# Transfers through DRAM in one piece, transposes that write with a stride, and a planner that counts transfers

## Chip, cores and metric

The kernel runs on one core of one Trainium2 chip. The metric is the device time in microseconds; "before" is the median of three runs. One more execution was taken with the hardware profiler, and all durations below come from it. TensorE (PE in the profile) multiplies; VectorE (DVE), ScalarE (ACT) and GpSimd (POOL) do elementwise work; SyncE (SP) issues nearly all DMAs.

## The reference

There are 128 graphs of 128 nodes with 512 features (`x`) and a weighted adjacency matrix each (`adj`, 128 x 128), all fp32. Four residual layers follow one another, each with a layer norm:

```
x = layernorm(x + L0(x, adj))   # T = row-normalised adj * exp(leaky_relu(s_j + s_i)); relu(x W0 + T x W1 + T T x W2 + b)
x = layernorm(x + L1(x, adj))   # hypergraph conv 512 -> 1024, relu, layer norm, hypergraph conv 1024 -> 512, plus x
x = layernorm(x + L2(x, adj))   # F = row-normalised exp(act(8 tanh(s_i + s_j))) * adj, times row sums of adj; F x W
x = layernorm(x + L3(x, adj))   # attention with 8 heads, scores times (adj + adj), output projection
```

Layer 0 needs T transposed, layer 1 needs adj and its hidden activations `h` transposed, layer 2 needs F transposed, layer 3 needs its input `x3` and the attention weights `S` transposed[...].

## The kernel before

The graphs are taken in 64 pairs (`U = 2`); a job of `layer0`, `layer1` or `layer23` works on two pairs. Weight products are done by a seven-product scheme (`strassen`, nested in `twice`); each product accumulates in a PSUM bank (`bank`, or `t0`, `t1`), which VectorE or ScalarE then adds or copies into SBUF before the bank is written again.

Nothing is issued in the order of the program text. Every call (`pe.matmul`, `ve.transpose`, `sp.dma_start` and so on) is recorded by `Plan.add` with a price in ns from `estimate`, a key (the layer's stage times `WHEN0`, `WHENT`, `WHENH` and the like) and its dependencies. `Plan.order` then plays the five engines forward in a list schedule: it gives tiles their buffers, lets an operation begin when its inputs and a buffer are there, counts `ISSUE` = 450 ns of SyncE for a DMA, and makes transfers follow one another through one pipe. `Plan.deadlines` works due times back from TensorE's starts, and `emit` plays the schedule up to two times more with these as ranks of all engines but TensorE, keeps the shortest, and emits every engine's instructions in that order. Each engine then runs its list in order. `plan.together(share)` makes one operation of several calls, at `share` of the summed price. As `emit` makes all calls at one line, the profile has almost everything under L375; operations are told apart by tile and shape.

A 128 x 128 transpose that isn't done on TensorE takes two steps. `through_dram` stores the source into a DRAM scratch tile, cut into four column blocks of 32 (index `k`), and its `load()` reads it back so that partition `32 k + r` holds column block `k` of some rows; `from_dram` does such a read directly from an input. Then `turned` transposes 32 x 32 blocks on VectorE. Rows come in the order `(m r)`: row 32 m + r, with four groups `m`.

- With `in_order=True` (`e` in layer 0, `h` in layer 1, `x3` in layer 3, whose scratch tiles the profile calls `e`, `h` and `x`) the store is issued in four DMAs of 32 partitions each per block `j`, so that DRAM holds rows as `k r m j w` and the loaded row is 32 m + r.
- With `False` (`F` in layer 2, `S` in attention) it is one DMA of 128 partitions per `j`; the load takes `(r m)`, row 4 r + m, and the rows are put in order later, when ScalarE copies the product out of PSUM (`rows_in_order`). The last attention job, whose `S` does not go through DRAM, is brought into that order by ScalarE copies that write with `"p (i m r) -> p i r m"`.
- `from_dram` (`x` in layer 0, `adj` in layer 1) issues four DMAs of 32 partitions for each of the two graphs of a pair, into `p m j w`.

Every transpose writes 32 neighbouring elements in a run. The functions that the change touches follow, with the line numbers of the profile.

Of the kernel before, what the change touches and what calls it, by code (L numbers as in the profile page):

```python
# [17 lines left out]
P = 128  # L18
D = 512
C = D // P  # L20
Q = 32
# [5 lines left out]
U = 2  # L27
# [33 lines left out]

LATENCY = ((0, 205, 215, 255, 300), (225, 120, 110, 200, 200), (160, 145, 140, 200, 200), (110, 140, 100, 105, 200),
           (2300, 2300, 2300, 2300, 2300))
ISSUE, BEGIN = 450, 1000
EARLY = -0.5
QW = 3 * P + 2
SLACK = 60
SPARE, AHEAD = 4, 6
YIELD = 20
SIZE = {"four": U * D, "sq": U * (P + 2), "bank": D, "col": 12, "row": D, "w28": 7168, "q7": 7 * 2 * P,  # L70
        "w7": 7 * QW, "out": U * 4 * QW, "t0": D, "t1": D, "row1": 4 * D, "k": U * (P + 2),
        "prep": U * D}
# [51 lines left out]
def estimate(engine, name, out, args, kw):  # L124

    n = out.idx.size if isinstance(out, View) else 0
    views = [a for a in args if isinstance(a, View)]
    psum = any(a.tile.kind in PSUM for a in views)
    scalars = sum(isinstance(a, View) and a.idx.size == 1 for k, a in [*enumerate(args), *kw.items()] if k != "accum_out")
    if engine == PE:  # L130
        return 107 if name == "transpose" else (1.74 if n <= P else 1.68) * n
    if name == "dma_start":
        return ISSUE
    if engine == DVE:
        if name == "bn_aggr":
            return 95
        if name == "reciprocal":
            return 67 + 6.5 * n
        if name in ("tensor_reduce", "bn_stats"):
            n = views[0].idx.size  # L140
        fast = name in ("tensor_scalar", "tensor_copy") and not psum and "accum_out" not in kw
        return 67 + n / (1.92 if fast else .96) + (61 * scalars if n > 8 else 0)
    if engine == ACT:
        return 50 + n / 1.2 + (0 if psum else 43) + 92 * scalars + 94 * ("accum_out" in kw)
    if name == "tensor_tensor":
        return 500 + 35 * n if OP.pow in args else 150 + 2.1 * n if n < 800 else 1.82 * n
    return 60 if name == "memset" else 180 + 3.2 * n if n > 8 else 215


def shares_port(engine, name, args, kw):  # L150
# [22 lines left out]
class Plan:  # L173
# [64 lines left out]
    def order(self, urgent=None):  # L238


        ops = self.ops
# [30 lines left out]
        come, free, start = [0.0] * n, [0.0] * 5, [0.0] * n  # L272
        port = [0.0] * 5
        pipe, reached = 0.0, EARLY
        for k in range(n):
            if not left[k]:
                ready[ops[k][0]][k] = 0.0

        def look(e):

            can = []
            soonest = math.inf
            for k, t in ready[e].items():
                if e == SP and ops[k][8] > reached and not ops[k][4]:
                    continue
                t = max(t, free[e], port[e] if ops[k][6] else 0)
                new = {}
                for tile in ops[k][5]:
                    if tile not in place:
                        new.setdefault(tile.kind, []).append(tile)  # L290
                for kind, tiles in new.items():
                    s, m = slots[kind], len(tiles)
                    spare = 0
                    if not all(tile in line[kind][-m:] for tile in tiles):
                        spare = SPARE if all(tile in line[kind][-m - AHEAD:] for tile in tiles) else math.inf
                    if len(s) < m + (min(spare, 4) if kind == "bank" else spare):
                        break
                    t = max(t, sorted(s)[m - 1][0])
                else:
                    can.append((rank[k], t, k))  # L300
                    if t < soonest:
                        soonest = t
            if not can:
                return None
            r, t, k = min(c for c in can if c[1] <= soonest + SLACK)
            return t, k
# [3 lines left out]
        while count < n:  # L310
# [15 lines left out]
            free[e] = end = t + o[2]  # L326
            if o[7]:
                end = pipe = max(pipe, t + BEGIN) + o[7]
            if e == PE and o[8] > reached:
                reached = o[8]  # L330
                stale.add(SP)
# [52 lines left out]
def kernel(  # L384
# [357 lines left out]
    def scratch(name, *shape):  # L742
        t = tc.dram_tile(list(shape), FP, name=name)
        return Tile("dram", t)
# [1 line left out]
    def part(tile, how, first, n=1):  # L746
        return View(tile, np.arange(first, first + n), (how,))

    def through_dram(src, name, in_order=True):


        _, nj, _, nw = src.shape
        d = scratch(name, 4, Q, 4, nj, nw) if in_order else scratch(name, 4, P, nj, nw)
        for j in range(nj):
            if in_order:
                with plan.together():
                    for m in range(4):
                        sp.dma_start(part(d, lambda t, m=m, j=j: t.rearrange("k r m j w -> m j r k w")[m, j], j),
                                     src[m * Q:(m + 1) * Q, j], run=nw, parts=Q)
            else:  # L760
                sp.dma_start(part(d, lambda t, j=j: t.rearrange("k p j w -> j p k w")[j], j), src[:, j], run=nw)

        def load():
            t = four().rearrange("p u f -> p (u f)") if nj * nw == U * P else sq().rearrange("p u n -> p (u n)")
            how = "k r m j w -> (k r) (m j w)" if in_order else "k (r m) j w -> (k r) (m j w)"
            sp.dma_start(t, part(d, lambda t: t.rearrange(how, m=4), 0, nj), run=4 * nj * nw)
            return t
        return load

    def from_dram(src, kind):  # L770

        nj, _, n = src.shape
        t = kind().rearrange("p u f -> p (u f)").rearrange("p (m j w) -> p m j w", m=4, j=nj)
        for j in range(nj):
            with plan.together():
                for k in range(4):
                    sp.dma_start(t[k * Q:(k + 1) * Q, :, j],
                                 src[j].rearrange("(m r) (k w) -> k r m w", r=Q, k=4)[k],
                                 run=n // 4, parts=Q)
        return t.rearrange("p m j w -> p (m j w)")  # L780

    def turned(dst, t):

        ve.transpose(dst.rearrange("p q (m r) -> p m q r", r=Q), t.rearrange("p (m q a) -> p m q a", m=4, a=Q))

    def turned_part(dst, t, q):

# [69 lines left out]
                pe.transpose(pt[:, b * P:(b + 1) * P], s, ident)  # L857
        return pt

    def pair_turned(load):  # L860
        t = sq()
        turned(t, load())
        return t

    def load_rows(src):
# [114 lines left out]
    def layer0(i0):  # L980
# [5 lines left out]
        xT, loads = [], []  # L986
        for xb in xbs:
            xT.append(four().rearrange("p u (c n) -> p u c n", n=P))
            turned(xT[-1].rearrange("p u c n -> p (u c) n"), xb)
        yield  # L990
        left = lefts(xT)
        yield
# [40 lines left out]
        for r, i in enumerate(both):  # L1033
            plan.key = base + WHENT[1][r]
            x0 = load_rows(x[i:i + U].rearrange("b p f -> p b f"))
            TT = pair_turned(loads[r])
            norm = layer_norms()
            for m in (1, 0):
                for b in range(U):
                    p = tile_of(("t0", "t1")[b], D)  # L1040
                    by = p.rearrange("p (q i) -> p q i", i=P)
                    to, of = (R[r][:, b, :, k * P:(k + 1) * P] for k in (m, m + 1))
                    ac.copy(by, to)
                    pe.matmul(by, TT[:, b], of, start=False, stop=True, skip_group_check=True)
                    if m:
                        ac.copy(to, by)
                    else:
                        ve.scalar_tensor_tensor(x0[:, b], p, 0.0, x0[:, b], op0=OP.max, op1=OP.add)
                        norm(x0[:, b])
                plan.key += .2  # L1050
            sp.dma_start(x1d[i // U], x0)
# [114 lines left out]
    def layer1(i0):  # L1166
# [4 lines left out]
        HTs, HBs = [], []  # L1171
        for (_, ab), in each(loaded):
            AT = sq()
            turned(AT, ab)
            HT = sq()
            cnt = col(U)
            for b in range(U):
# [73 lines left out]
        for r, i in enumerate(both):  # L1251
            plan.key = base + WHENH[r]
            hT = []
            for b in range(U):
                t = four().rearrange("p g (c n) -> p g c n", n=P)
                turned(t.rearrange("p g c n -> p (g c) n"), loads[U * r + b]())
                hT.append(t)
            ops = operands(hT[0][:, 0], hT[0][:, 1], hT[1][:, 0], hT[1][:, 1])
            plan.key = base + WHENW[r]
# [107 lines left out]
    def layer23(i0):  # L1367
# [10 lines left out]
        for i, x2, A in each(both, x2s, As):  # L1378
# [15 lines left out]
            ve.reciprocal(r, r)  # L1394
            for b in range(U):
                po.tensor_scalar(F[:, b], F[:, b], r[:, b:b + 1], deg[:, b:b + 1], op0=OP.mult, op1=OP.mult)
            FTs.append(through_dram(F.rearrange("p b (k w) -> p b k w", w=Q), f"F{i}", False))
        yield
        opss = []
        for load, x2 in each(FTs, x2s):  # L1400
# [20 lines left out]
        xT = []  # L1421
        for load, in each(loads):
            xT.append(four().rearrange("p u (c n) -> p u c n", n=P))
            turned(xT[-1].rearrange("p u c n -> p (u c) n"), load())
        yield
        left = lefts(xT)
        yield
# [28 lines left out]
    def attention(i0, A, qT, kT, v, x3d, base, r):  # L1456
# [4 lines left out]
        Ss = [four().rearrange("p u (j a) -> p (u j) a", a=Q).rearrange("p (k j) a -> p k j a", k=4)  # L1461
              for _ in range(U)]
        ps = [[bank(), bank()] for _ in range(U)]
        with plan.together(.65):
            for b in range(U):
                for i in range(C):
                    for r2 in range(2):
# [4 lines left out]
        for b in range(U):  # L1472
# [14 lines left out]
                to = Ns[b].rearrange("p u (j k a) -> p (u j) k a", k=4, a=Q).rearrange("p j k a -> p k j a")  # L1487
            po.tensor_tensor(to, S, ssum[:, None, :, None].to_broadcast([P, 4, HEADS, Q]), OP.mult)
            if not last:
                loads.append(through_dram(S.rearrange("p k (x j) a -> p x k (j a)", x=1), f"S{i0 + b}", False))  # L1490
        plan.key = base + WHENP[r]
        for b in range(U):
            PT = four()
# [10 lines left out]
            PTs.append(PT)  # L1504
        cT = four().rearrange("p u (i n) -> p u i n", n=P)
        ps = [bank() for _ in range(U)]
        with plan.together(.62):
            for b in range(U):
                for i in range(C):
                    for r2 in range(2):  # L1510
# [76 lines left out]
```

## Time and profile before

| | us |
|---|---|
| median of 3 runs (5395.81 to 5402.33) | 5396.24 |
| the profiled execution | 5406.97 |
| its span, first to last instruction | 5405.0 |
| TensorE busy / VectorE busy / GpSimd busy | 5324.9 / 4410.1 / 3913.6 |

Layer 0 fills about the first 1340 us, layer 1 runs to about 3050, layers 2 and 3 together to the end. The DMA engines are busy 49% of the span on SyncE's queue, with 842412 packets and 813.70 MB; 269612 of the packets are under 512 bytes. The busy table gives for a stretch of time each engine's busy us with the number of its instructions. A row of groups gives the operation, out<-in by tile names, shapes, the count, busy us, the mean ns of one, and then the idle time of that engine just ahead of these instructions with what ended it. "issue" in the chain of waits is time in which nothing seen was waited for. Because matmuls are pipelined and their ends modelled, TensorE's busy share says only that something was in flight.

### The profile page before, as it was taken

How to read it: one execution, taken by the hardware profiler on the slowest of the kernel's cores; microseconds unless marked ns; L12 is line 12 of the kernel's file. 1: busy time of each engine (PE TensorE's matmuls, PEld its weight loads, DVE VectorE, ACT ScalarE, POOL GpSimd, SP SyncE). 2: the span in 40 equal slices, each digit the busy share in tenths (PEclk: the TensorE clock that was granted, in tenths of full speed). 3: DMA queues.
4: the chain of work that ended last, by engine and by line, in shares of the span. 5: the costliest groups of instructions: out<-in, count | busy, mean ns of one | idle time of the engine just before them, and what ended most of it. 6: DMA issues, size and time to landing. Idle time of an engine off the chain costs nothing.

```text
span 5405.0 us, 93824 instructions
## 1 busy us (share of the span) xinstructions
PE 5324.9 (99%) x29039; PEld 4239.3 (78%) x29039; DVE 4410.1 (82%) x11721; ACT 2387.5 (44%) x6085; POOL 3913.6 (72%) x4937
## 2 busy tenths in 40 slices
PE   8999999999999999999999999999999999999998
PEld 4555555555788888888888889988988998998987
DVE  7788888887888888888888777878777878788886
ACT  3343333343444444444444444444444444444444
POOL 6777677676676767676767577777777777778776
PEclk9999999999999999999999999999999999999999
DMA  4444444435554545454554745555555555555543
GB/s 112 134 135 130 130 146 134 128 113 181 154 157 145 158 146 158 147 157 146 157 150 146 246 137 158 159 154 161 162 154 158 157 161 156 162 154 163 156 153 109
DMA packets 842412, 813.70 MB, mean 151 GB/s; under 512 B 269612, under 2 KB 642868, under 8 KB 841912
## 3 DMA queue, kind: packets, MB, share of 16 engines
q1 hardware_dynamic: 838914, 806.65, 49.2%
q8 instruction: 231, 3.78, 0.3%
q14 instruction: 269, 2.20, 0.1%
q10 hardware_dynamic: 2998, 1.06, 0.1%
HBM read 458.38 MB, written 349.04 MB: 149 GB/s over the span
## 4 chain that ended last, share of the span: by engine, by line
PE 87%; DVE 5%; DMA 3%; issue 1%; SPq 1%; ACT 1%; POOL 1%; ACTq 0%; DVEq 0%; POOLq 0%
PE bank L375 66%; PE t L375 21%; DVE out L375 1%; SPq L375 1%; DVE col L375 1%; DVE four L375 1%; DMA first<-x3d 1%; DMA four<-in_x_dram 1%; ACT out L375 0%; DMA out<-x3d 0%; DMA sq<-e 0%; POOL out L375 0%; DVE junk L375 0%; DVE first L375 0%; DMA sq<-in_adj_dram 0%
## 5 line engine op out<-in xcount | busy, mean ns | idle before, releaser
L375 PE MATMUL bank<-first,four 128*128 128x386 f32 (+2 forms) x6008 | 1735.6, 433 | 27.3 <-DVE out L375 11.4
L375 PEld LDWEIGHTS bank<-first,four 128*128 128x128 f32 (+1 forms) x6008 | 1073.0, 189 | 600.6 <-DVE out L375 119.2
L375 DVE TENSOR_TENSOR out<-bank,out 128x386 f32<-128x386 f32 (+1 forms) x2089 | 1011.2, 501 | 261.6 <-PE bank L375 197.3
L375 DVE TENSOR_TENSOR four<-bank,four 128x256 f32<-128x256 f32 x1285 | 529.5, 418 | 204.6 <-PE bank L375 176.6
L375 POOL TENSOR_TENSOR col<-col,neghalf 128x2 f32<-128x2 f32 x320 | 233.9, 731 | 374.6 <-DVE col L375 372.5
L375 POOL TENSOR_TENSOR out<-out 128x772 f32<-128x772 f32 (+3 forms) x233 | 328.0, 1416 | 219.4 <-DVE out L375 187.5
L375 POOL TENSOR_TENSOR four<-four 128x256 f32<-128x256 f32 (+2 forms) x448 | 362.5, 822 | 171.6 <-DVE four L375 110.4
L375 PE MATMUL bank<-first,out 128*128 128x256 f32 (+1 forms) x1912 | 458.6, 375 | 10.4 <-DVE four L375 6.2
L375 POOL TENSOR_TENSOR four<-four,four 128x256 f32<-128x256 f32 (+2 forms) x501 | 436.2, 876 | 11.7 <-DVE four L375 3.7
L375 ACT COPY out<-bank 128x258 f32<-128x258 f32 (+2 forms) x523 | 208.2, 403 | 481.6 <-PE bank L375 415.2
L375 PEld LDWEIGHTS bank<-first,out 128*128 128x128 f32 (+1 forms) x1912 | 340.6, 187 | 77.4 <-DVE four L375 13.1
L375 ACT ACTIVATE four<-four,col,col 128x512 f32<-128x512 f32 (+1 forms) x300 | 263.6, 905 | 153.8 <-POOL col L375 139.1
L375 PE MATMUL bank<-four,first 128*128 128x256 f32 (+3 forms) x1680 | 303.4, 324 | 6.9 <-DVE out L375 3.0
L375 PE MATMUL bank<-out,first 128*128 128x128 f32 (+2 forms) x1636 | 269.3, 300 | 2.5 <-DVE out L375 2.2
L375 PEld LDWEIGHTS bank<-four,first 128*128 128x128 f32 (+2 forms) x1680 | 237.8, 182 | 34.7 <-DVE out L375 5.4
L375 PE MATMUL t<-out,sq 128*128 128x512 f32 x512 | 258.0, 596 | 6.7 <-ACT t L375 4.8
L375 ACT ACTIVATE out<-out,col,col 128x512 f32<-128x512 f32 (+1 forms) x191 | 166.7, 901 | 193.6 <-POOL col L375 193.6
L375 ACT COPY t<-out 128x512 f32<-128x512 f32 x256 | 151.0, 591 | 225.5 <-DVE four L375 150.7
L375 DVE BATCH_NORM_STATS2 col<-four 128x6 f32<-128x512 f32 x368 | 244.7, 679 | 4.1 <-ACT four L375 1.7
L375 DVE TENSOR_TENSOR four<-t,four 128x256 f32<-128x256 f32 x435 | 181.4, 418 | 80.5 <-PE t L375 72.2
L375 PEld LDWEIGHTS bank<-out,first 128*128 128x128 f32 (+1 forms) x1636 | 224.9, 187 | 21.8 <-DVE out L375 2.6
L375 PE MATMUL t<-first,four 128*128 128x256 f32 (+1 forms) x902 | 232.5, 377 | 0.2 <-DVE four L375 0.2
(535 smaller groups left out, 13056.6 us busy)
## 6 DMA issues: line engine op xcount, KB each, us to landing
four<-h SPq DMA_DIRECT2D x72, 512.0 KB, 5.3
h<-four SPq DMA_DIRECT2D x272, 128.0 KB, 2.5
four<-in_x_dram SPq DMA_DIRECT2D x504, 64.0 KB, 2.1
four<-in_x_dram SPq DMA_DIRECT2D x61, 512.0 KB, 4.3
x1d<-four SPq DMA_DIRECT2D x61, 512.0 KB, 2.9
four<-x1d SPq DMA_DIRECT2D x61, 512.0 KB, 4.4
out<-x1d SPq DMA_DIRECT2D x54, 512.0 KB, 4.8
first<-S SPq DMA_DIRECT2D x54, 512.0 KB, 4.3
```

What stands on the lines that cost most here:

```text
L375: call(*map(real, args), **{n: real(a) for n, a in kw.items()})
```

## The change

`through_dram` loses `in_order`: every store is one DMA of all 128 partitions per `j`, and every load takes rows as 4 r + m. What was put in order by the four stores is now put in order by VectorE: `turned_back` transposes with the output pattern `"p q (r m) -> p m q r"`, so that 32 elements in succession are written 4 elements apart. It is used for `e`, `h` and `x3`. `from_dram` reads both graphs of a pair in one DMA per column block, four in all, into `(j m) w`, and `turned_two` transposes that layout with runs of 32 as before. The planner's SyncE may issue a transfer only when the eighth before it has landed (`LANES`, `LANDED`), and several of its prices are changed.

```diff
-ISSUE, BEGIN = 450, 1000
+ISSUE, BEGIN, LANES, LANDED = 450, 1000, 8, 2050
-YIELD = 20
+YIELD = 0
 @@ estimate()
-        return 67 + n / (1.92 if fast else .96) + (61 * scalars if n > 8 else 0)
+        slow = 118 if "accum_out" in kw and not psum else 0
+        return 67 + n / (1.92 if fast else .96) + (61 * scalars if n > 8 else 0) + slow
-    return 60 if name == "memset" else 180 + 3.2 * n if n > 8 else 215
+    return 60 if name == "memset" else (740 - 160 * scalars if scalars else 180 + 3.2 * n) if n > 8 else 215
 @@ Plan.order()
+        landed = [0.0] * LANES
+                if e == SP:
+                    t = max(t, *(landed[j - LANES] - ISSUE * j for j in range(len(ops[k][1]))))
+                landed += [end + LANDED] * len(o[1])
+                landed = landed[-LANES:]
 @@ through_dram()
-        d = scratch(name, 4, Q, 4, nj, nw) if in_order else scratch(name, 4, P, nj, nw)
+        d = scratch(name, 4, P, nj, nw)
         for j in range(nj):
-            if in_order:
-                with plan.together():
-                    for m in range(4):
-                        sp.dma_start(part(d, lambda t, m=m, j=j: t.rearrange("k r m j w -> m j r k w")[m, j], j),
-                                     src[m * Q:(m + 1) * Q, j], run=nw, parts=Q)
-            else:
-                sp.dma_start(part(d, lambda t, j=j: t.rearrange("k p j w -> j p k w")[j], j), src[:, j], run=nw)
+            sp.dma_start(part(d, lambda t, j=j: t.rearrange("k p j w -> j p k w")[j], j), src[:, j], run=nw)
 @@ load()
-            how = "k r m j w -> (k r) (m j w)" if in_order else "k (r m) j w -> (k r) (m j w)"
+            sp.dma_start(t, part(d, lambda t: t.rearrange("k (r m) j w -> (k r) (m j w)", m=4), 0, nj), run=4 * nj * nw)
 @@ from_dram()
-        for j in range(nj):
-            with plan.together():
-                for k in range(4):
-                    sp.dma_start(t[k * Q:(k + 1) * Q, :, j], src[j].rearrange("(m r) (k w) -> k r m w", r=Q, k=4)[k],
-                                 run=n // 4, parts=Q)
+        with plan.together():
+            for k in range(4):
+                sp.dma_start(t[k * Q:(k + 1) * Q], bass.AP(tensor=src.tensor, offset=src.offset + k * w,
+                                                           ap=[[n, Q], [Q * n, 4 * nj], [1, w]]), run=w, parts=Q)
+    def turned(dst, t, how="p q (m r) -> p m q r"):
+        ve.transpose(dst.rearrange(how, r=Q), t.rearrange("p (m q a) -> p m q a", m=4, a=Q))
+    def turned_back(dst, t):
+        turned(dst, t, "p q (r m) -> p m q r")
+    def turned_two(dst, t):
+        ve.transpose(dst.rearrange("p (j q) (m r) -> p j m q r", j=U, r=Q),
+                     t.rearrange("p (j m q a) -> p j m q a", j=U, m=4, a=Q))
 @@ layer0: x with turned_two, e with turned_back;  layer1: adj with turned_two, h with turned_back;  layer23: x3 with turned_back
 @@ attention()
-        with plan.together(.65):
+        with plan.together(.558):
-        with plan.together(.62):
+        with plan.together(.531):
```

More of the change, by code (lines that the diff above doesn't have):

```diff
@@ L747, in part, with through_dram @@
         return View(tile, np.arange(first, first + n), (how,))
-    def through_dram(src, name, in_order=True):
+    def through_dram(src, name):
         _, nj, _, nw = src.shape
-        d = scratch(name, 4, Q, 4, nj, nw) if in_order else scratch(name, 4, P, nj, nw)
+        d = scratch(name, 4, P, nj, nw)
         for j in range(nj):
-            if in_order:
-                with plan.together():
-                    for m in range(4):
-                        sp.dma_start(part(d, lambda t, m=m, j=j: t.rearrange("k r m j w -> m j r k w")[m, j], j),
-                                     src[m * Q:(m + 1) * Q, j], run=nw, parts=Q)
-            else:
-                sp.dma_start(part(d, lambda t, j=j: t.rearrange("k p j w -> j p k w")[j], j), src[:, j], run=nw)
+            sp.dma_start(part(d, lambda t, j=j: t.rearrange("k p j w -> j p k w")[j], j), src[:, j], run=nw)
         def load():
             t = four().rearrange("p u f -> p (u f)") if nj * nw == U * P else sq().rearrange("p u n -> p (u n)")
-            how = "k r m j w -> (k r) (m j w)" if in_order else "k (r m) j w -> (k r) (m j w)"
-            sp.dma_start(t, part(d, lambda t: t.rearrange(how, m=4), 0, nj), run=4 * nj * nw)
+            sp.dma_start(t, part(d, lambda t: t.rearrange("k (r m) j w -> (k r) (m j w)", m=4), 0, nj), run=4 * nj * nw)
             return t
@@ L770, in from_dram @@
     def from_dram(src, kind):
-        nj, _, n = src.shape
-        t = kind().rearrange("p u f -> p (u f)").rearrange("p (m j w) -> p m j w", m=4, j=nj)
-        for j in range(nj):
-            with plan.together():
-                for k in range(4):
-                    sp.dma_start(t[k * Q:(k + 1) * Q, :, j],
-                                 src[j].rearrange("(m r) (k w) -> k r m w", r=Q, k=4)[k],
-                                 run=n // 4, parts=Q)
-        return t.rearrange("p m j w -> p (m j w)")
-    def turned(dst, t):
-        ve.transpose(dst.rearrange("p q (m r) -> p m q r", r=Q), t.rearrange("p (m q a) -> p m q a", m=4, a=Q))
+        nj, rows_, n = src.shape
+        w = n // 4
+        t = kind().rearrange("p u f -> p (u f)").rearrange("p (m w) -> p m w", m=4 * nj)
+        with plan.together():
+            for k in range(4):
+                sp.dma_start(t[k * Q:(k + 1) * Q], bass.AP(tensor=src.tensor, offset=src.offset + k * w,
+                                                           ap=[[n, Q], [Q * n, 4 * nj], [1, w]]), run=w, parts=Q)
+        return t.rearrange("p m w -> p (m w)")
+    def turned(dst, t, how="p q (m r) -> p m q r"):
[5 more added lines that the diff above has]
+                     t.rearrange("p (j m q a) -> p j m q a", j=U, m=4, a=Q))
     def turned_part(dst, t, q):
@@ L858, in spread_pair, with pair_turned @@
         return pt
-    def pair_turned(load):
+    def pair_turned(load, how=turned):
         t = sq()
-        turned(t, load())
+        how(t, load())
         return t
@@ L988, in layer0 @@
             xT.append(four().rearrange("p u (c n) -> p u c n", n=P))
-            turned(xT[-1].rearrange("p u c n -> p (u c) n"), xb)
+            turned_two(xT[-1].rearrange("p u c n -> p (u c) n"), xb)
         yield
@@ L1035, in layer0 @@
             x0 = load_rows(x[i:i + U].rearrange("b p f -> p b f"))
-            TT = pair_turned(loads[r])
+            TT = pair_turned(loads[r], turned_back)
             norm = layer_norms()
@@ L1173, in layer1 @@
             AT = sq()
-            turned(AT, ab)
+            turned_two(AT, ab)
             HT = sq()
@@ L1255, in layer1 @@
                 t = four().rearrange("p g (c n) -> p g c n", n=P)
-                turned(t.rearrange("p g c n -> p (g c) n"), loads[U * r + b]())
+                turned_back(t.rearrange("p g c n -> p (g c) n"), loads[U * r + b]())
                 hT.append(t)
@@ L1396, in layer23 @@
                 po.tensor_scalar(F[:, b], F[:, b], r[:, b:b + 1], deg[:, b:b + 1], op0=OP.mult, op1=OP.mult)
-            FTs.append(through_dram(F.rearrange("p b (k w) -> p b k w", w=Q), f"F{i}", False))
+            FTs.append(through_dram(F.rearrange("p b (k w) -> p b k w", w=Q), f"F{i}"))
         yield
@@ L1423, in layer23 @@
             xT.append(four().rearrange("p u (c n) -> p u c n", n=P))
-            turned(xT[-1].rearrange("p u c n -> p (u c) n"), load())
+            turned_back(xT[-1].rearrange("p u c n -> p (u c) n"), load())
         yield
@@ L1489, in attention @@
             if not last:
-                loads.append(through_dram(S.rearrange("p k (x j) a -> p x k (j a)", x=1), f"S{i0 + b}", False))
+                loads.append(through_dram(S.rearrange("p k (x j) a -> p x k (j a)", x=1), f"S{i0 + b}"))
         plan.key = base + WHENP[r]
```

## The prediction

> **What bounds the kernel now.** I read the engine totals, the busy table by stage, the VectorE groups kept apart by shape, the waits by stage and one stretch of the chain of waits, in that order.
>
> ```profile
> PE 5324.9 (99%) x29039; PEld 4239.3 (78%) x29039; DVE 4410.1 (82%) x11721; ACT 2387.5 (44%) x6085; POOL 3913.6 (72%) x4937
> ...
> 1320.00:1400.00 80.00, 72.76 (x327) 54.62 (x327) 61.07 (x204) 36.63 (x71) 55.40 (x83) 0.94 0.62 195
> 1400.00:2950.00 1550.00, 1540.28 (x7409) 1308.93 (x7408) 1342.21 (x3709) 728.26 (x1209) 1058.61 (x1442) 1.00 0.51 153
> ...
> 3100.00:5220.00 2120.00, 2106.57 (x15491) 1907.23 (x15491) 1693.40 (x4447) 958.64 (x3272) 1638.79 (x2002) 1.00 0.51 157
> ```
>
> The first row is the whole span; in the others the columns after the length are PE, PEld, DVE, ACT, POOL, the granted clock, the DMA share. TensorE has a matmul in flight 99% of the span: 80 us of 5405 are idle, 9.7 in the middle of layer 1 (1400 to 2950) and 13.4 in layers 2 and 3 (3100 to 5220). The 80 are the ceiling of any gain in waits, and by the same table 32 of them lie in the first 60 and the last 55 us. VectorE comes next: in layer 1 it is busy 1342 of 1550 us, 87%, with 208 us to spare; in layers 2 and 3 80%, with 427 to spare.
>
> ```profile
> L375 DVE STREAM_TRANSPOSE four<-four 128x1024 f32<-128x1024 f32 x116 | 142.6, 1230 | 3.4 <-DMA first<-in_L_gnn_Wk_dram 3.0 <-DVE sq L375 0.2
> L375 DVE STREAM_TRANSPOSE sq<-sq 128x256 f32<-128x256 f32 x192 | 83.4, 434 | 17.9 <-DMA sq<-in_adj_dram 7.5 <-DMA sq<-e 4.5 <-DMA four<-h 2.2
> ...
> L375 ACT COPY out<-bank 128x512 f32<-128x512 f32 x3 | 3.0, 1067 | 0.0
> L375 ACT COPY four<-bank 128x512 f32<-128x512 f32 x3 | 3.2, 1080 | 0.0
> L375 ACT COPY rows<-bank 128x512 f32<-128x512 f32 x3 | 1.6, 577 | 0.3 <-PE bank L375 0.3
> ```
>
> A block transpose of 1024 columns takes 1230 ns, of 256 columns 434, and it hardly ever waits for a DMA. The last three rows are ScalarE in the last 60 us: the third is its ordinary copy of 512 columns, 577 ns. The first two are the copies of the last attention job, which write with neighbouring elements 32 apart (`"p (i m r) -> p i r m"`): 1067 and 1080 ns. It is the one strided write to SBUF that I found in this trace.
>
> ```profile
> L375 SPq DMA_DIRECT2D e<-sq x512: 302/430/1889, 54.3 to 1358.2; - x171
> ...
> PE t L375 <- ACT t L375: 3.4, 1, 3.4
> ...
> 1324.70 9.64 DMA sq<-e
> 1334.35 0.02 issue
> ...
> 1336.24 5.59 DMA first<-w2s
> 1341.83 0.02 issue
> 1341.85 10.73 DMA out<-x1d
> ```
>
> SyncE's issue costs 430 ns (median). Transfers end TensorE's waits in few places: around 594 us, where a late `in_x_dram` load leads through VectorE and ScalarE to a TensorE wait of 3.4 us, and at the change from layer 0 to 1 (the chain's pieces above), where TensorE idles 7.2 of 80 us at a clock of 0.94.
>
> [...] `S`, one store of 512 KB, lands after 3.2 us; `h`, the same bytes in four, takes 3 x 0.46 + 2.5 = 3.9.
>
> **Part by part.** *Transfers.* Stores of `e` and `x` go from 8 issues to 2 a pair, those of `h` from 8 to 2 (two batch entries), the reads of `x` and `adj` from 8 to 4. With 64 pairs that is 64 x (6 + 6 + 6 + 4 + 4) = 1664 issues fewer, x 0.43 = 716 us off SyncE's queue. No bytes, runs or packets change. Issues in one group are 0.46 us apart (1.85 us for four of `in_adj_dram` in the timeline). To landing: `h` 3.9 to `S`'s 3.2; `x` 7 x 0.46 + 1.8 = 5.0 to about 0.46 + 2.9 (between 2.5 and 3.2); `e` 7 x 0.46 + 1.5 = 4.7 to `F`'s 0.46 + 3.6 = 4.1, or 5.3 with `F`'s upper figures; reads 5.3 to about 3 x 0.46 + 2.8 = 4.2. About 1 us earlier each, all hidden behind TensorE's queue of work, since the transposes wait almost nowhere; if that cover went, each would be worth its 1 us. Where it counts I give 3 us for 594, 4 for the change of layers and 2 for the start (SyncE's eight `in_x_dram` issues stand ahead of weights there): -9 us, bounds 0 and -25.
>
> *Transposes.* `turned_back` writes neighbouring elements 4 apart, 16 bytes[...]. VectorE shows no such write. Lower bound: nothing. Upper: ScalarE's excess, (1074 - 577)/512 = 0.97 ns an element, hence 0.99 us on 1024 columns and 0.25 on 256. I take the upper value[...]. A gain is excluded: the same elements are written. Layer 1 has 128 such transposes (`h`): +127 us. Layer 3 has 64 (`x3`): +63. Layer 0 has 64 of 256 columns (`e`): +16. `turned_two` keeps runs of 32: nothing.
>
> *What of it reaches TensorE.* VectorE evicts PSUM in its queue's order, and each eviction stands behind the transpose; the next product into that bank waits for it. Layer 1's spare of 208 us would fall to about 90, VectorE to 94%. Of the 208, some 140 are waits for TensorE (usable slack), the rest waits for other engines. Products come every 0.87 us (timeline: two accumulating 256-column steps), so a lone delay of 1 us fits in the free banks; two transposes back to back, with evictions behind them, don't. I take a third of 127 as reaching TensorE: +42 (bounds 0 and 127). Layer 3 at 80%: a tenth of 63, +6 (0 to 40). Layer 0's queue hides its 16 (0 to 16).
>
> *Planner.* `LANES`, `YIELD`, the prices of accumulating VectorE and scaled GpSimd instructions and the shares .558 and .531 change no instruction; they change the order on all five queues. The matmul count is unchanged. The shares fit the trace better: an attention group of 32 half-array matmuls takes 32 x 62 ns (start to start in the trace) = 1984, .558 x 1.74 x 128 x 16 = 1988. But the planner still prices a transpose at 67 + 1024/.96 = 1134 ns, so it would not see the new delay. With 23 us idle in the two long stages I value the reordering at 0, bounds -10 and +15.
>
> **Sum:** -9 + 42 + 6 + 0 = +39 us. The profiled execution took 5407.0 us, its span 5405.0 and 2.0 around it; it becomes about 5446. It stands 10.7 over the median, so against 5396.2: **5435**, slower by 0.7%.
>
> **Rivals.** *A: strided writes are free on VectorE* (the ScalarE rows are another engine, at 128 bytes). Then only the repairs are left: 5396 - 9 - up to 6 from better order = 5381 to 5387. For it: 29 of the 80 idle us (17.6 in the first 60, 4.6 between 540 and 630, 7.2 at the change of layers) lie where loads take part in the wait. Against: in each of these stretches other waits stand beside the load. It decides where less than the 9 us of repairs leaks, a fifth of what I forecast: 0.07 us for each of layer 1's transposes. *B: hidden or balanced:* excess below 0.3 us a transpose, or VectorE's waits for TensorE swallow it: 5396 +/- 10. *C: VectorE becomes layer 1's bound:* the 68 us that aren't waits for TensorE can't be used, and much of the 140 comes back after every eviction as a round trip, so that only a quarter of the excess is hidden: 5396 - 9 + 95 + 6 = 5488. The pairs speak for it, the 9.7 us idle of today's TensorE against it. *D: order alone is worse*, transposes unchanged: 5410.
>
> **How the numbers follow.** Forecast 0.40, C 0.11, D 0.04: slower 0.55. B 0.18. A 0.27, mostly just beyond the line at 5385: 0.2%, 11 us, is about what a measurement of this kernel can tell from no change. The range reaches from A with the upper bound of the repairs (5396 - 25) to a little past C: 5372 to 5500; the bounds of 127 and 40 together (5554) are left out.
>
> **What would show it.** The 1024-column transposes split in two groups: `S`'s stay at 1230 ns, those of `h` and `x` at about 2200 (A: all 1230). VectorE's busy sum rises by 150 to 210 us; layer 1's TensorE idle goes from 10 to some 50 us, released by VectorE; SyncE has 1664 DMA instructions fewer. If the transposes show 2200 and layer 1's idle stays at 10 us, my leak is wrong; if they show 1230, my main step is.

## The result, and the profile after

The changed kernel takes 5460.1 us (median of four runs, 5458.7 to 5462.2) against 5397.8 before in the same comparison: a ratio of 1.0117, 95% interval 1.0104 to 1.013. It is 62 us slower. The profiled execution's span is 5458.7 us.

The engine totals of the changed kernel, and its busy table by stage (after the length: PE, PEld, DVE, ACT, POOL with their instruction counts, the clock, the DMA share, GB/s):

```profile
PE 5352.8 (98%) x29039; PEld 4234.2 (78%) x29039; DVE 4559.6 (84%) x11721; ACT 2406.8 (44%) x6085; POOL 3922.2 (72%) x4937
...
1320.00:1400.00 80.00, 74.68 (x365) 59.22 (x363) 64.96 (x206) 44.54 (x80) 59.18 (x93) 1.00 0.56 176
1400.00:2950.00 1550.00, 1523.91 (x7249) 1273.94 (x7249) 1383.90 (x3630) 718.96 (x1182) 1036.54 (x1411) 1.00 0.46 150
...
3100.00:5220.00 2120.00, 2094.21 (x15244) 1886.95 (x15243) 1724.21 (x4375) 948.85 (x3202) 1611.90 (x1965) 1.00 0.48 155
```

The counts say more than the busy time: in layer 1's window TensorE started 7249 matmuls where it was 7409 before, 2.2% fewer, while its idle time rose by 16 us only (1550 less 1523.9 is 26.1, before 9.7). 2.2% of 1550 us is 34 us, so about half of what was lost does not show as idle time: busy time only says that something was in flight. The change of layers (first stretch) is better than before: 5.3 us idle at a granted clock of 1.00, before 7.2 at 0.94.

VectorE's transposes in layer 1 of the changed kernel, and the tile view of `e`'s transfers:

```profile
L381 DVE STREAM_TRANSPOSE four<-out 128x1024 f32<-128x1024 f32 x29 | 59.6, 2057 | 0.0
L381 DVE STREAM_TRANSPOSE four<-four 128x1024 f32<-128x1024 f32 x27 | 55.8, 2067 | 0.0
...
L381 DVE STREAM_TRANSPOSE sq<-sq 128x256 f32<-128x256 f32 x57 | 24.8, 435 | 0.6 <-DMA sq<-in_adj_dram 0.6
...
L381 SPq DMA_DIRECT2D e<-sq x128: 359/367/1293, 55.9 to 1327.3; - x128
...
DMA to landing us min/median/max: 1.8/2.1/7.1
```

`h`'s transposes take 2057 and 2067 ns where 1230 was; those of `adj` (`turned_two`, runs of 32) are unchanged at 435. Over the trace the strided ones take about 2060 ns on average at 1024 columns and 640 at 256: 0.81 ns an element more, 128 x 0.83 + 64 x 0.83 + 64 x 0.21, about 172 us. SyncE issues 2714 DMAs where it was 4378, the 1664 fewer that were counted. `e`'s stores went from 512 to 128 and land after 2.1 us.

To say where time is won or lost, two landmarks serve that every version has: the start of the last 386-column matmul (end of layer 0's products) and of the last 130-column one (`HT` by `HB`, near the end of layer 1; in the changed kernel 9 of `h`'s 128 transposes come after it). From the traces, in us (the kernels are those of the experiments below):

| kernel | to the first | between | from the second to the end of the span |
|---|---|---|---|
| before | 1330.6 | 1627.5 | 2446.9 |
| changed | 1319.4 | 1656.6 | 2482.7 |
| changed, runs (a1) | 1314.6 | 1615.9 | 2434.3 |
| before, strided (b1) | 1323.2 | 1685.8 | 2496.4 |
| changed, price told (t1) | 1316.3 | 1628.1 | 2437.6 |
| changed, `x3` in runs (x1) | 1317.8 | 1658.9 | 2441.4 |
| changed, stride of 2 (s2) | 1317.3 | 1614.8 | 2434.6 |
| before, planner edits (p1) | 1322.7 | 1625.9 | 2443.7 |
| before, merged reads (r1) | 1322.3 | 1615.8 | 2443.1 |
| planner edits and merged reads (c1) | 1315.5 | 1613.1 | 2432.0 |
| two half stores (v2, its profiled run) | 1315.0 | 1619.5 | 2480.4 |

The profiled execution of before lay some 10 us over its median, so distances to it in this table are by that much too favourable to the others; the versions' medians below are not affected.

### The profile page after: what moved, and what is told of

Same layout as the page of the kernel before. It is cut to its first block, busy times and chain, and to the rows that moved or that the text cites. A ratio compares the mean times of both kernels' runs of the same rounds, so it can differ in the third digit from the quotient of the medians.

```text
span 5458.7 us, 91621 instructions
## 1 busy us (share of the span) xinstructions
PE 5352.8 (98%) x29039; PEld 4234.2 (78%) x29039; DVE 4559.6 (84%) x11721; ACT 2406.8 (44%) x6085; POOL 3922.2 (72%) x4937
## 4 chain that ended last, share of the span: by engine, by line
PE 68%; DVE 21%; issue 5%; POOL 4%; ACT 1%; DMA 1%; SPq 0%; DVEq 0%; ACTq 0%; POOLq 0%
PE bank L381 52%; PE t L381 16%; DVE four L381 6%; DVE col L381 4%; DVE out L381 4%; DVE first L381 2%; DVE bank L381 1%; POOL four L381 1%; DVE junk L381 1%; DVE side L381 1%; POOL out L381 1%; ACT four L381 1%; POOL col L381 1%; DVE rows L381 1%; DVE sq L381 1%
## 5 line engine op out<-in xcount | busy, mean ns | idle before, releaser
L381 DVE TENSOR_TENSOR out<-bank,out 128x386 f32<-128x386 f32 (+1 forms) x1897 | 931.2, 510 | 235.2 <-PE bank L381 179.4
L381 ACT ACTIVATE four<-four,col,col 128x512 f32<-128x512 f32 (+1 forms) x396 | 337.6, 883 | 368.9 <-POOL col L381 356.4
L381 PE MATMUL bank<-first,out 128*128 128x256 f32 (+2 forms) x1760 | 411.3, 370 | 7.7 <-DVE four L381 2.9
L381 PE MATMUL bank<-four,first 128*128 128x128 f32 (+3 forms) x2944 | 392.8, 288 | 3.9 <-DVE rows L381 1.5
L381 PEld LDWEIGHTS bank<-four,first 128*128 128x128 f32 (+2 forms) x2944 | 341.2, 187 | 30.3 <-issue 10.0
L381 PEld LDWEIGHTS bank<-first,out 128*128 128x128 f32 (+2 forms) x1760 | 300.9, 184 | 71.6 <-DVE four L381 11.7
L381 DVE TENSOR_TENSOR first<-bank,first 128x256 f32<-128x256 f32 (+1 forms) x562 | 235.1, 421 | 119.9 <-PE bank L381 101.8
L381 ACT COPY four<-bank 128x256 f32<-128x256 f32 (+1 forms) x402 | 181.1, 452 | 325.9 <-PE bank L381 308.5
L381 PE MATMUL bank<-out,first 128*128 128x256 f32 (+3 forms) x1368 | 268.0, 331 | 4.8 <-DVE four L381 2.1
L381 PE MATMUL bank<-first 128*128 128x128 f32 (+2 forms) x1664 | 235.7, 278 | 3.4 <-DVE four L381 3.1
```

The costliest lines, as they stand in the source:

```text
L381: call(*map(real, args), **{n: real(a) for n, a in kw.items()})
```

## The experiments

The theory was that the strided writes alone make the kernel slower, and that all else gains a little. The main rival was that the new order of the queues is worse.

**Runs again in the changed kernel (a1).** The order of every queue is that of the changed kernel; the rows then come out permuted, which nothing puts right.

```diff
     def turned_back(dst, t):
-        turned(dst, t, "p q (r m) -> p m q r")
+        turned(dst, t)
```

> The changed kernel with every engine's list in the same order, but turned_back writes runs of 32 as before the change (the rows of e, h and x3 then stay in the order 4r+m, which is not put right: left out). Strided-write theory: the transposes fall from 2060 to 1230 ns and from 640 to 430, VectorE's sum by 172 us, and the time to 5380 to 5396, at or a little below before (the planner's repairs of 9 us stay). Rival, the new order is itself the worse one: VectorE falls the same, but the time stays above 5430. Mixed: between 5396 and 5430, in that proportion.

Measured: 5367.8 us, 0.9948 of before (0.9935 to 0.996), 12 us below the range expected. The rest of the change gains 29 us, three times what was expected of it, and the strides cost 92. The rival is out. By the landmarks the 94 us between the two spans are 4.8 in layer 0, 40.7 in layer 1 and 48.4 after it.

As both traces hold the same instructions in the same order, each can be compared with itself. An eviction is a VectorE or ScalarE instruction that takes a product out of its PSUM bank (`<-bank` or `<-t`). VectorE and TensorE around one transpose of `x3`, first with runs, then strided:

```profile
3980.31 1.24 DVE L381 STREAM_TRANSPOSE four<-first 128x1024 f32<-128x1024 f32 x1
3981.47 0.39 DVE L381 TENSOR_TENSOR first<-bank,first 128x256 f32<-128x256 f32 x1
3981.78 0.42 DVE L381 TENSOR_TENSOR four<-bank,four 128x256 f32<-128x256 f32 x1
3982.29 0.42 DVE L381 TENSOR_TENSOR first<-bank,first 128x256 f32<-128x256 f32 x1
...
3982.01 0.61 PE L381 MATMUL t<-first 128*128 128x128 f32 x4
3982.46 1.03 PE L381 MATMUL bank<-four,four 128*128 128x256 f32 x4
```

```profile
4050.05 2.06 DVE L381 STREAM_TRANSPOSE four<-first 128x1024 f32<-128x1024 f32 x1
4051.94 0.42 DVE L381 TENSOR_TENSOR first<-bank,first 128x256 f32<-128x256 f32 x1
4052.27 0.42 DVE L381 TENSOR_TENSOR four<-bank,four 128x256 f32<-128x256 f32 x1
4052.60 0.42 DVE L381 TENSOR_TENSOR first<-bank,first 128x256 f32<-128x256 f32 x1
...
4051.75 0.61 PE L381 MATMUL t<-first 128*128 128x128 f32 x4
4052.74 1.13 PE L381 MATMUL bank<-four,four 128*128 128x256 f32 x4 [0.38 <-DVE four L381]
```

With runs, two evictions follow the transpose back to back, 0.31 us apart; with the third, 0.51 us later, VectorE has caught up with TensorE, which goes on without a gap. Strided, the evictions still follow 0.33 us apart at the third: the second comes 2.22 us after the transpose's start where it was 1.47, and the product that needs the bank starts 0.99 us after its neighbour where it was 0.45: 0.54 us lost. Over the 68 places of this kind after the second landmark, nearly all with a lone transpose, VectorE is about 0.7 us late 2 us after the start of the transpose, and TensorE hardly late after 2 us, 0.52 after 3 and 0.55 after 5. In layer 1, over 74 places with one or two transposes, VectorE is about 0.8 late after 4 us, TensorE 0.4 after 8; places with a lone transpose and places with two cost TensorE the same there, 0.37 each.

**Strides in the kernel before (b1).** `turned_back` is added as in the change and used in three places of three functions; the order of every queue is that of the kernel before.

```diff
-            TT = pair_turned(loads[r])
+            TT = pair_turned(loads[r], turned_back)
 ...
-                turned(t.rearrange("p g c n -> p (g c) n"), loads[U * r + b]())
+                turned_back(t.rearrange("p g c n -> p (g c) n"), loads[U * r + b]())
 ...
-            turned(xT[-1].rearrange("p u c n -> p (u c) n"), load())
+            turned_back(xT[-1].rearrange("p u c n -> p (u c) n"), load())
```

> The kernel before, same transfers and same order of every queue, with the strided output pattern in the transposes of e, h and x3 and nothing else (their rows come out in a permuted order, which nothing puts right). Strided-write theory: +172 us of VectorE, of which the old order lets 40 to 80 reach the end: 5440 to 5480. Rival, the new order is the worse one: the old order, with 208 us spare on VectorE in layer 1, hides them: 5396 to 5415.

Measured: 5507.7, 1.0207 of before (1.0193 to 1.0221), so +111 us, beyond the expected end. The old order hides no more than the new one: by the landmarks 58 us are lost in layer 1 and 50 after it.

**The stages apart (x1):** the changed kernel with `turned` for `x3` alone.

> The changed kernel in the same order, with the transposes of x3 alone writing runs (its rows stay out of order), those of e and h strided. By the course of the two traces of one order, layers 2 and 3 lost 49 us to 53 us of longer transposes: 5460 - 49 = 5411, within 8. If layer 3's loss is really delay carried over from layer 1's transposes or their buffers, it stays above 5440.

Measured: 5417.2 (1.0038, 1.0024 to 1.0051), 43 us off the changed kernel. The last stage falls to 2441.4 and layer 1 stays at 1658.9, so the loss after layer 1 belongs to `x3`'s transposes but for some 7 us. Of their 53 us more, 43 reach the end, 81%; those of `e` and `h` cost the other 49 of the 92.

**A step of two elements (s2).**

```diff
     def turned_back(dst, t):
-        turned(dst, t, "p q (r m) -> p m q r")
+        ve.transpose(dst.rearrange("p q (h r m) -> p h m q r", h=2, m=2),
+                     t.rearrange("p (h m q a) -> p h m q a", h=2, m=2, a=Q))
```

> The changed kernel in the same order, with neighbouring elements of e, h and x3 written 2 apart (8 bytes) in place of 4 (16 bytes); the rows then come out in another order, which nothing puts right. [...] transposes of 1230 ns and 5368, or about 1640 and 5405 to 5420. If any stride costs the same: 2060 ns and 5460.

Measured: 5366.6 (0.9944, 0.993 to 0.9958), the time with runs. The transposes of layer 1 in this kernel:

```profile
L381 DVE STREAM_TRANSPOSE four<-out 128x1024 f32<-128x1024 f32 x31 | 38.2, 1234 | 0.0
L381 DVE STREAM_TRANSPOSE four<-four 128x1024 f32<-128x1024 f32 x28 | 34.7, 1239 | 0.0
L381 DVE STREAM_TRANSPOSE out<-four 128x1024 f32<-128x1024 f32 x22 | 27.2, 1236 | 0.0
```

With a step of 8 bytes these transposes took 1234 to 1239 ns, with runs (a1) 1231 to 1236; with a step of 16 bytes (the changed kernel) 2055 to 2067, 0.81 ns an element more. Why one step costs this and the other doesn't was not shown, and a step of 12 bytes was not tried.

**The planner is told the price (t1).**

```diff
+        if name == "transpose" and out.idx.flat[1] - out.idx.flat[0] > 1:
+            return 67 + n / .96 + .81 * n
         fast = name in ("tensor_scalar", "tensor_copy") and not psum and "accum_out" not in kw
```

> The changed kernel, whose planner now prices a transpose with a strided output at 0.81 ns an element more (829 ns on 1024 columns), what the trace of the changed kernel shows; nothing else. The order may change, the instructions don't. Theory 'the leak comes from an order that does not know the price': much of the 92 us comes back, 5370 to 5410. Rival 'no room behind a transpose, whatever the order': VectorE's 172 us more still delay evictions, 5430 to 5465.

Measured: 5382.0 (0.9971, 0.996 to 0.9982). Its busy table by stage, and the largest group of strided transposes in layer 1:

```profile
1400.00:2950.00 1550.00, 1537.40 (x7389) 1300.31 (x7390) 1401.68 (x3698) 731.09 (x1205) 1048.41 (x1436) 1.00 0.47 151
3100.00:5220.00 2120.00, 2101.76 (x15593) 1912.10 (x15593) 1727.52 (x4465) 970.87 (x3313) 1627.97 (x2004) 1.00 0.49 158
...
L383 DVE STREAM_TRANSPOSE four<-four 128x1024 f32<-128x1024 f32 x30 | 61.4, 2046 | 0.0
```

The transposes still take about 2060 ns, and VectorE is busier in layer 1 than in the changed kernel (1401.7 of 1550) as more work gets through; yet 78 of the 92 us are back. So VectorE's capacity was not what was short; the order made the difference.

Where the 78 us come from can be estimated from the traces: give each shape of matmul its median time from start to start in c1 (216 ns for 256 columns, 112 for 128), and add up by how much TensorE falls behind this in the 5 us from each strided transpose's start. In layer 1 that is 30 us in the changed kernel, 2 in a1 and 3 in t1: there the told price removes the loss where it arose. After the second landmark it is 41, 2 and 28. Yet t1's whole stage there is only 3 us longer than a1's (the table), so it makes up elsewhere for most of what the transposes still cost; whether the price does that, or any other order would have, is not shown. Nor is it shown what the new order does differently: an eviction stands directly behind the strided transposes of 1024 columns in 161 of 192 cases, in the changed kernel in 116.

**Where the 29 us come from (p1, r1, c1).** p1 is the kernel before with the planner's edits alone, r1 with `from_dram` and `turned_two` alone, c1 with both; all three keep the four stores and plain transposes.

> The kernel before with the planner's edits alone (LANES, LANDED, YIELD 0, the new prices and shares); transfers and transposes as before. Strided-write theory: within 0.3% of before, 5385 to 5400, with the late load at 594 us and the change from layer 0 to 1 repaired or not. Rival, the new order is worse: 5420 or more. VectorE's busy sum stays at 4410 in both.

> The kernel before with the reads of x and adj merged (four transfers a pair in place of eight, turned_two), its planner and its stores as before. The planner's edits alone gave 5395, planner and merged reads 5358. If the merged reads are the gain by themselves: 5355 to 5370. If they need the planner that counts transfers in flight: 5385 to 5400.

> The changed kernel without strided writes and correct: the planner's edits and the merged reads of x and adj with turned_two stay; e, h and x3 go back to four stores of 32 partitions and plain transposes. Strided-write theory: 5380 to 5396, like the changed kernel with runs, and at least as fast as before. If fewer stores are worth something by themselves, it stands some us over that kernel. Rival, the new order is worse: 5430 or more.

Measured: p1 5395.3 (0.9998, 0.999 to 1.0007), as expected; r1 5384.1 (0.9976, 0.9967 to 0.9985), a microsecond under the range given for reads that need the new planner; c1 5358.3 (0.9933, 0.9921 to 0.9946), 22 us below its range. c1 is the fastest of all, 38 us under before. Alone the planner's edits gain 1.5 us and the merged reads 13; together they gain 38. One part of what p1 lacks can be seen at the change of layers, in its waits of TensorE (us in all, times, longest) and SyncE's timeline:

```profile
PE bank L381 <- POOL sq L381: 10.0, 1, 10.0
...
1339.18 4.62 SPq L381 DMA_DIRECT2D e<-sq  x8
1343.85 3.75 SPq L381 DMA_DIRECT2D sq<-in_adj_dram  x8
1347.69 0.38 SPq L381 DMA_DIRECT2D sq<-e  x1
1348.11 4.38 SPq L381 DMA_DIRECT2D sq<-in_adj_dram  x9
```

The reads of `adj` stand in eights on SyncE behind `e`'s stores; TensorE waits 10.0 us once for the work on them. In c1 the reads are fours, and the longest wait of TensorE in these 80 us is 0.6. That is 10 of the 32 us between the spans of p1 and c1; 12 more lie after the second landmark and are not traced to a cause. Which of the planner's edits it is that helps the merged reads was not measured. c1 and a1 differ in the stores and in the order: c1, with four small stores, is 9.5 us faster, so merging stores isn't shown to be worth anything.

**Half stores, strides of two (v2).** `e`, `h` and `x3` are stored as row 64 h + 2 r + m in two transfers of 64 partitions, and transposed with a step of 2.

> A correct version with free strides: the changed kernel in which e, h and x3 are stored in two transfers of 64 partitions (row 64h + 2r + m) and transposed with neighbouring elements 2 apart; twice the store transfers of the changed kernel, half of those of the kernel with merged reads. Strided-write theory: transposes at 1235 ns and 5360 to 5375, like the changed kernel with strides of two. If fewer stores are worth something beside merged reads: below 5358, the time of the kernel with merged reads and four stores. If orders scatter by some 10 us: anywhere from 5355 to 5380.

Measured: 5411.4 (1.0028, 1.0018 to 1.0039); in the run with its profile 5418.2, beside 5402.5 of before. That is a miss: 45 us over s2. Its transposes take 1235 ns and layer 1 is only 5 us longer than in s2; the excess, 46 us, lies after it. TensorE's waits, and one of them in the timeline, with VectorE's instructions ahead of it:

```profile
PE bank L381 <- DVE rows L381: 16.7, 13, 1.4
PE bank L381 <- DVE first L381: 13.3, 12, 2.4
...
3655.35 0.69 DVE L381 BATCH_NORM_STATS2 col<-four 128x6 f32<-128x512 f32 x1
3655.95 1.23 DVE L381 STREAM_TRANSPOSE ks<-four 128x1024 f32<-128x1024 f32 x1
3657.10 0.39 DVE L381 TENSOR_TENSOR first<-t,first 128x256 f32<-128x256 f32 x1
...
3657.54 1.13 PE L381 MATMUL t<-side,first 128*128 128x256 f32 x4 [1.36 <-DVE first L381]
```

The eviction that TensorE waits for stands behind a transpose of 1.23 us and a statistics instruction of 0.69 us ahead of that. The same wait, 1.31 to 1.37 us with the same two instructions ahead of the eviction, comes 24 times, every 73 us from 3439 to 5125: 32 of the 46 us. In s2 TensorE has no wait over 0.7 us in that stretch. `x3`'s transposes waited for a DMA 2.3 us in all. So here too it is the order: a product that waits for an eviction behind a 1.2 us transpose. Why the planner arrives at it is not shown.

It limits what p1, r1, c1, t1 and the 29 us of a1 against before say, for there the order differs too, and v2 shows that an order can cost 32 us. How far small changes of the planner scatter was not measured. The 92 us of the strides, b1, x1 and s2 are free of this: each has the order of the kernel that it is compared with.

## Why the prediction was right, and where it was not

The forecast was +39 us, the result +62, from the mechanism named. By its own terms:

- *Price of a strided write.* Taken from ScalarE: 0.99 us on 1024 columns, 0.25 on 256. Measured 0.83 and 0.21; 172 us in place of 206. The upper value was the right choice, a fifth too high; that VectorE would pay what ScalarE does was the author's estimate, as no row of VectorE before showed it. VectorE's busy time rose by 149.5 us, just under the 150 to 210 given. Busy time counts overlapping instructions once: against a1 it rises by 134 us, the sum of all durations by 177.
- *Leak in layer 1.* +42 predicted, 40.7 measured by the landmarks: some 40% of about 100 us rather than a third of 127. That the number fits is luck, for the reason given isn't borne out: two transposes back to back were to leak and lone ones not, and both cost TensorE 0.37 us a place. What was right is that the planner would not see the new delay (t1).
- *Leak after layer 1.* +6 predicted, 48.4 measured by the landmarks, of which x1 puts 41 down to `x3`. This is the term that failed. "Layer 3 at 80%: a tenth of 63" read the room behind a transpose from the stage's mean. The two timelines show evictions directly behind the transpose and a product that starts within 0.3 us of the end of the second one, so 81% of 53 us reached the end. "A lone delay of 1 us fits in the free banks" was wrong: a lone 0.83 us made TensorE 0.55 late.
- *Layer 0.* 0 predicted, 4.8 measured.
- *Repairs.* -9 predicted with bounds 0 and -25, -29 measured (a1), outside them. The wait at 594 us is gone (TensorE busy 89.6 of the 90 us from 540 on, before 85.4) and the change of layers is shorter, as named. The rest comes from the merged reads and the reordering, put at 0, together (c1); how much is whose stays open. The two wrong terms pull in opposite directions, +42 and -20: that the total came within 23 us is in part luck.
- *TensorE's idle time in layer 1.* "Some 50 us" was predicted and 26 came, though the stage lost what was forecast: the marker was ill chosen.
- *Transfers.* The count was right. The packets were to stay and fell from 842412 to 815773. To landing, `h` took 3.3 us (3.2 predicted) and `e` 2.1 (3.6). Stores and reads were early enough, as said.
- *Rivals.* A fell on 2060 ns, B on the size. C, VectorE as layer 1's bound, is contradicted by t1. D, a worse order with unchanged transposes, is contradicted by a1.

## What to carry to other kernels

Price an access pattern by the nearest row that has the same pattern, even on another engine (here 0.97 ns an element from ScalarE, 0.81 measured on VectorE), and then look at what stands directly behind the instruction: with evictions behind it for whose banks products waited, most of the delay was passed on here (81%, in a stage whose VectorE was busy 80% of the time). A planner that orders by prices must get the new price along with the new instruction; here that edit alone was worth 78 us, part of which may be the luck of an order. An fp32 transpose of 1024 columns on VectorE took 1236 ns here when written with a step of 8 bytes (1230 in runs), and 2060 with 16 bytes. Measure a loss by landmarks or matmul counts, not by idle time (in layer 1 here 16 us of 34).

## What the runs showed of the hardware that was not expected

VectorE's block transpose of 1024 fp32 columns took 1236 ns when it wrote with a step of 8 bytes (s2), 1230 in runs (before) and 2060 with 16 bytes (the changed kernel). That last is 0.81 ns more for an element, less than the 0.97 of ScalarE's copies at a step of 128 bytes (before), and 256 columns took about as much more for an element (640 ns against 434).
